# A new prologue for a fused graph-attention and hypergraph kernel on one core

## The chip, the cores and the metric

The kernel runs on one core of a Trainium2 chip. The metric is the device time of one execution in microseconds (us), lower is better. The engines are named as in the profile: PE (TensorE matmul), PEld (its weight loads), DVE (VectorE), ACT (ScalarE), POOL (GpSimd), SP (SyncE, which here only issues DMAs). "SPq" and "ACTq" are the queues that issue DMAs.

## What is computed

For 128 graphs of 128 nodes and 512 features, two layers, all in float32:

```
# layer 0: graph attention with 8 heads of 64 units
feats   = einsum(x, W)                       # per head
e       = leaky_relu(e_self[i] + e_neigh[j], 0.2) + (-1e10) * (1 - adj)
out     = relu(softmax(e) @ feats + b)       # heads side by side
x       = layernorm(x + out)
# layer 1: two hypergraph convolutions, H = (adj != 0), w = first row of adj
conv(v, W, b) = D^-1 H B^-1 H^T (v @ W^T) + b
h       = layernorm(relu(conv(x, W1, b1))) * gamma + beta
x       = layernorm(x + conv(h, W2, b2) + x)
```

e_self and e_neigh are dot products of each head's features with a_self and a_neigh. Since features are x times W, both can be had from x and a "score weight" (W times a_self, W times a_neigh): 16 extra columns.

## The kernel before

**Tiling.** A work item is a pair of graphs; there are 64 pairs (`PAIRS`). Nodes lie on the 128 partitions. Products of the later pairs (`feature`, `hidden`, `weigh`) combine the two graphs and the two halves of a weight in a seven-product (Strassen-like) scheme, `chain`; the weights therefore have derived blocks (`second_sums`, `prepare_hidden`, `prepare_output_block_sums`). Matmuls go in two column tiles of 64 (`columns`, L97).

**Order.** Everything is issued in one order that is written out by hand. Each step of a pair has a lag and a due time inside a period (`step`, `at`); the list `todo` adds preparation steps; `first` overrides due times of single steps of the first pairs; the whole list is sorted by due time (L1232) and issued in that order. [...] There are eight PSUM banks (`bank`), taken in turn. Due times are a sorting key only, in a unit of the author's.

**Steps of one pair.** Load adj, its first row, x and 32x32 blocks of both; `nodes` (inverse node degrees, L360 to L369) and `write_nodes`/`spread_nodes` (through DRAM to all partitions); `mask` (adj to 0 or -1e10, POOL L378); `x_transpose`; features (`pf`); `spread_rows` (the scores, one column per head, are turned into rows L542 and written to DRAM, `rd`) and `neighbours` (read back, spread over all partitions, `nb` L570); `masked` (POOL L589, adds the mask); `leaky` (ACT L605), `largest` (DVE L611), `exponential` (ACT L619), each per graph g and half of the heads q; `e_write`, `e_read` (through DRAM, `ed` and `eb`) and `e_transpose` (DVE L640); `attend` (`pav`, L677, L703), `attended`; `add_bias` (POOL L742, adds b0 to the features); `residual`, `rstds` (root on POOL, L767), `first_shift`/`first_output` (normalisation on ACT, L785 to L794); `edges`, `scale_edges`, `propagator` (`pd`), `r_evict` (`R`): the matrix D^-1 H B^-1 H^T; `propagate` (`pz`), `z_evict` (ACT L829), `z_sums` (POOL L840); `hidden` (`phX`, `phY`, `phW`), `h_sum` (DVE L866), `relu`, `square`; `weigh` (`py`), `y_scale`, `output` (`pq`), statistics and store.

**The prologue before.** Pairs 0 and 1 take other steps. w0 comes as four blocks; `prepare_first` copies each into a tile with two more columns per head, and fills these: the block times the broadcast a_self (DVE, L234) or a_neigh (POOL, L234), reduced per head on DVE (L238). x of both pairs is transposed on PE (`x_transpose_first`, L397, `px`), and `plain_features` (L523, `pf`) multiplies 264 columns per half: features and scores together. Pair 0's scores go through DRAM like those of all pairs (L550, L570). The transposes of pair 0's exponentials are on PE (L651, `pet`). `prepare_output` (L276, `pv`: 16 matmuls of two rows by 256 columns), `prepare_output_sums`, `prepare_output_spread` (L288, `gw` and `bw`) give sums that fold gamma, beta and the mean into w2; `prepare_output_blocks` (L300, 16 operations on DVE) scales w2 in place. pv, gw and bw stand ahead of `pz` of pair 0; half of L300 is done before or during it.

## Time and profile before

| what | value |
|---|---|
| runs | 2393.14, 2398.22, 2399.10 us; median 2398.22 |
| the profiled execution's own time | 2395.3 us |
| its span, first to last instruction | 2393.4 us |
| mean granted clock of PE | 0.996 |
| first transposes of x | 8.08 us |
| rows of pair 0 made, and read back on all partitions | 20.72 us, 27.94 us |
| first leaky of pair 0; last block of pav | 29.24 us; about 40.7 us |
| pz of pair 0, first product of phX | 47.23 us, 50.69 us |
| pfX of pair 2, pav of pair 1, pz of pair 1 | 64.92, 74.46, 87.06 us |
| HBM read and written | 239.08 MB, 102.73 MB |

How to read it: in the page, shares are of the span; the stretches give busy time per engine between two times; a chain of waits starts at the last instruction and is followed back, so that it names at each time the work that was last. A line of the timeline gives start, duration, engine, source line, operation, tile written <- tile read, shape and count, and in brackets the idle time of the engine before it with what ended it. fp32 matmuls appear as two passes (an x8 is four matmuls), transposes as one. L97 is the helper `columns`, so its rows are told apart by tile names.

### The profile page before, as it was taken

Reading aid. Unit: us, or ns where it says so; the run is one execution under the profiler, and the core shown is the slowest. Engines: PE = TensorE matmul, PEld = TensorE weight load, DVE = VectorE, ACT = ScalarE, POOL = GpSimd, SP = SyncE. Lnnn points to the kernel's source line nnn. Section 1 sums busy time; section 2 is a strip of 40 time slices with the busy share of each in tenths; the row PEclk is TensorE's granted clock in tenths of the full one; section 3 lists DMA queues with packets and bytes.
Section 4 is the critical chain, followed back from the end, with each engine's and each line's share of the span. In section 5 each row is a group of like instructions: output and inputs, shape, how many; then the busy total and the mean of one; then the engine's idle time right before and its main releaser. Section 6 shows DMA issues by size and latency. Waiting matters only on the chain.

```text
span 2393.4 us, 80729 instructions
## 1 busy us (share of the span) xinstructions
PE 2360.8 (99%) x32309; PEld 2026.8 (85%) x32309; DVE 2089.6 (87%) x4456; ACT 1528.5 (64%) x4481; POOL 1825.6 (76%) x2060
## 2 busy tenths in 40 slices
PE   7899999999999999999999999999999999999998
PEld 6788887888888888888888888888888888888886
DVE  7989888898898898898898888988988988988975
ACT  4565765756667667667667666666676676676662
POOL 5877786777877877877877778778778778778774
PEclk9999999999999999999999999999999999999999
DMA  6555454555554555555545555544545555555541
GB/s 197 133 148 150 143 144 134 159 143 147 151 148 144 149 148 148 151 143 154 144 142 157 141 147 155 146 146 147 150 143 153 147 150 139 148 156 140 149 128 37
DMA packets 431134, 347.09 MB, mean 145 GB/s; under 512 B 151440, under 2 KB 380328, under 8 KB 430760
## 3 DMA queue, kind: packets, MB, share of 16 engines
q1 hardware_dynamic: 427288, 337.46, 49.5%
q8 instruction: 256, 4.19, 0.7%
q10 hardware_dynamic: 3472, 4.47, 0.6%
q14 instruction: 118, 0.97, 0.2%
HBM read 239.08 MB, written 102.73 MB: 143 GB/s over the span
## 4 chain that ended last, share of the span: by engine, by line
PE 89%; DMA 4%; DVE 3%; ACT 1%; POOL 1%; issue 1%; SPq 1%; DVEq 0%; POOLq 0%; ACTq 0%
PE phX L97 17%; PE pyX L97 17%; PE pfX L97 8%; PE pyW L97 8%; PE phW L97 8%; PE pav L703 5%; PE phY L97 4%; PE pz L97 4%; PE pfW L97 4%; PE pq L97 4%; PE pyY L97 4%; PE pfY L97 2%; DMA ed<-nb 1%; PE pd L97 1%; DMA nb<-rd 1%
## 5 line engine op out<-in xcount | busy, mean ns | idle before, releaser
L344 ACT COPY py<-pyX 128x257 f32<-128x257 f32 x189 | 70.7, 374 | 538.5 <-PE pyX L97 465.6
L97 PEld LDWEIGHTS phX<-zS,w_sb 128*64 128x64 f32 x6144 | 350.6, 137 | 36.3 <-POOL ft L742 23.1
L97 PE MATMUL phX<-zS,w_sb 128*64 128x128 f32 x6144 | 373.4, 273 | 2.6 <-ACT ph L344 2.6
L904 POOL TENSOR_TENSOR sq<-sq 128x512 f32<-128x512 f32 (+2 forms) x384 | 343.9, 896 | 20.1
L589 POOL TENSOR_TENSOR nb<-nb,neg 128x512 f32<-128x512 f32 x256 | 319.9, 1284 | 23.1 <-DMA nb<-rd 12.7
L605 ACT ACTIVATE nb<-nb,ft 128x128 f32<-128x128 f32 x1020 | 325.1, 392 | 13.7 <-POOL nb L589 13.7
L619 ACT ACTIVATE nb<-nb,nm 128x128 f32<-128x128 f32 x1024 | 319.4, 392 | 4.2 <-DVE nm L611 4.0
L767 POOL TENSOR_TENSOR rso<-veo,mhalf 128x2 f32<-128x2 f32 x63 | 44.2, 701 | 338.4 <-DVE veo L765 338.4
L97 PE MATMUL pyX<-w_sb,hS 128*64 128x257 f32 x2016 | 245.1, 380 | 0.0
L97 PE MATMUL pyX<-w_sb,h 128*64 128x257 f32 x2016 | 243.7, 379 | 0.5 <-ACT py L344 0.5
L97 PE MATMUL pyW<-w_sb,hS 128*64 128x256 f32 x2016 | 243.3, 378 | 0.0
L881 ACT ACTIVATE h<-h,vecs 128x128 f32<-128x128 f32 x768 | 239.4, 394 | 2.0 <-DVE h L866 1.4
L611 DVE TENSOR_REDUCE nm<-nb 128x4 f32<-128x512 f32 x256 | 175.2, 684 | 48.8 <-ACT nb L605 46.2
L97 PEld LDWEIGHTS pyX<-w_sb,h 128*64 128x64 f32 x2016 | 173.7, 136 | 46.2 <-ACT py L344 0.9
L97 PEld LDWEIGHTS pyW<-w_sb,hS 128*64 128x64 f32 x2016 | 174.7, 136 | 43.6 <-issue 0.3
L742 POOL TENSOR_TENSOR ft<-ft,b_bc 128x512 f32<-128x512 f32 x128 | 203.9, 1613 | 6.1 <-ACT ft L533 6.1
L97 PEld LDWEIGHTS pyX<-w_sb,hS 128*64 128x64 f32 x2016 | 168.7, 137 | 38.7 <-issue 0.8
L640 DVE STREAM_TRANSPOSE eT<-eb 128x512 f32<-128x512 f32 x252 | 163.5, 685 | 5.7 <-DMA eb<-ed 4.7
L805 DVE SCALAR_TENSOR_TENSOR o<-y,b_bc 128x512 f32<-128x512 f32 x128 | 164.7, 1325 | 0.0
L1006 DVE SCALAR_TENSOR_TENSOR y<-y,rsh,bw_bc 128x512 f32<-128x512 f32 x126 | 150.1, 1229 | 14.9 <-POOL rsh L1002 14.9
L469 POOL TENSOR_TENSOR hS<-h 128x512 f32<-128x512 f32 x126 | 162.1, 1287 | 0.0
L892 ACT ACTIVATE sq<-h 128x512 f32<-128x512 f32 x256 | 160.6, 629 | 2.1
(178 smaller groups left out, 5672.4 us busy)
## 6 DMA issues: line engine op xcount, KB each, us to landing
nb<-rd SPq DMA_DIRECT2D x127, 512.0 KB, 5.6
ed<-nb SPq DMA_DIRECT2D x126, 512.0 KB, 3.4
eb<-ed SPq DMA_DIRECT2D x504, 128.0 KB, 2.9
x<-in_x_dram SPq DMA_DIRECT2D x64, 512.0 KB, 4.0
out_dram<-o SPq DMA_DIRECT2D x63, 512.0 KB, 2.9
xb<-in_x_dram SPq DMA_DIRECT2D x248, 128.0 KB, 5.5
a<-in_adj_dram SPq DMA_DIRECT2D x64, 128.0 KB, 2.4
w<-in_adj_dram SPq DMA_DIRECT2D x128, 64.0 KB, 5.0
```

The lines of the kernel that those rows point to most:

```text
L97: nc.tensor.matmul(to[rows], lhs[:, rows], rhs, start=start, stop=stop, skip_group_check=True)
L469: engine.tensor_tensor(t[:, i], in0, in1, op=op)
L589: nc.gpsimd.tensor_tensor(t, t, neg[:, :, None, :].to_broadcast([P, NB, HH, B]), op=ALU.add)
L605: nc.scalar.activation(t, t, AF.Prelu, bias=s["ft"][:, g, h, 0:1], alpha=SLOPE)
L611: nc.vector.tensor_reduce(s["nm"][:, g, hs], scores(p, s, g, hs).rearrange("p b h j -> p h b j"), AX.XY, ALU.max, negate=True,)
L619: nc.scalar.activation(t, t, AF.Exp, bias=s["nm"][:, g, h:h + 1])
L640: nc.vector.transpose(s["eT"][:, g, hs, :].rearrange("p h (b i) -> p h b i", b=NB), s["eb", g][:, :, hs, :].rearrange("p b h j -> p h b j"),)
L742: nc.gpsimd.tensor_tensor(t, t, b0_bc.rearrange("p (h u) -> p h u", h=H), op=ALU.add)
L805: nc.vector.scalar_tensor_tensor(s["o"][:, g, :], s["y"][:, g, :], 2.0, b2_bc, op0=ALU.mult, op1=ALU.add)
L881: nc.scalar.activation(dst[:, k, :], src[:, k, :], AF.Relu, bias=b1_sb[:, c:c + 1])
L892: nc.scalar.activation(s["sq"][:, g, q * KH // 2:(q + 1) * KH // 2, :], hid(s, g, q), AF.Square, scale=DH ** -0.5,)
L904: nc.gpsimd.tensor_tensor(t[:, :n, :], t[:, :n, :], t[:, n:2 * n, :], op=ALU.add)
```

## The change

Only steps of the first pairs and of the constants change; loops over pairs 2 to 63 stay as they are (apart from `blocked`, which loses the special layout of pair 0).

1. **Loads.** gamma, beta, b1, a_self and a_neigh come as 32 rows on ACT's queue; adj and its first rows of pair 0 first on SP, then w0 in four pieces of full rows, then x of pair 0 per graph. b0, w1, w2, the first row of pair 1 and the blocks of pair 2 are issued behind `spread_nodes` of pair 0, all on SP (before: w2 and half of w1 on ACT).
2. **Score weights.** w0 is transposed on PE (`first_transpose`), multiplied by a block matrix made of a_self and a_neigh in column tiles of 32 (`first_scores`), turned back (`first_scores_turn`) and added up by one reduction (`first_scores_out`). The copies of w0 into the wide tile and its four sums go from ACT and DVE to POOL.
3. **Scores as rows.** `x_scores` multiplies the score weights by x transposed, in four column tiles; `x_scores_turn` turns them into columns for the bias of `leaky`. `score_spread` puts pair 0's rows on all partitions by a matmul with a selection matrix (`heads`), and `first_masked` adds the mask while leaving PSUM. Pair 0 no longer goes through DRAM. Pair 1's rows still do, on ACT's queue.
4. **Attention of pair 0** is written out per graph and half; `first_root` and `first_normalize` take the root per graph and normalise on DVE instead of ACT.
5. **Features** of pairs 0 and 1 are products of 512 columns straight from `w0_raw`; two products of pair 1's graph 0 and all four of graph 1 stand after its attention scores, the last four behind `pz` of pair 0.
6. **Constants.** pv goes into four column tiles of 32 rows and stands behind pz and those features, its copy goes to ACT; gw stands behind phX's and phY's first products, bw behind the next; the 16 operations that scale w2 stand together behind gw.

The core of the diff:

```diff
+    for ap in (gamma, beta, b1, a_self, a_neigh):
+        rows = ap.rearrange("(k p) -> k p", p=P)
+        nc.scalar.dma_start(vec_rows[at_row:at_row + rows.shape[0]], rows)
+    load(0)
+    for k in range(KF):
+        load_first(k)
...
-            for c, bc in enumerate((as_bc, an_bc)):
...
-                (nc.vector, nc.gpsimd)[c].tensor_tensor(
-                    t, raw, bc[:, j * QU:(j + 1) * QU].rearrange("p (h u) -> p h u", h=HH)
-                    [:, None].to_broadcast([P, KF // 2, HH, U]), op=ALU.mult,
-                )
-                nc.vector.tensor_reduce(dst[:, :, :, c], t, AX.X, ALU.add)
...
+    def first_scores(k):
...
+        for c in range(KF):
+            nc.tensor.matmul(
+                made["pwa"][c * B:(c + 1) * B, k * P:(k + 1) * P], w0_a[:, c * B:(c + 1) * B],
+                made["wT", k // 2][:, k % 2, c], start=True, stop=True, skip_group_check=True,
+            )
...
     def prepare_first_sums():
-        second_sums(nc.vector, [w0_sb[:, i] for i in range(7)], w0_12)
+        second_sums(nc.gpsimd, [w0_sb[:, i] for i in range(7)], w0_12)
...
+        for n in range(2):
+            for j in range(2):
+                for c in range(NB):
+                    k = 2 * c + n
+                    blk = w2_blocks[2 * (k // (KH // 2)) + j][0]
+                    nc.tensor.matmul(
+                        t[c * B:(c + 1) * B, j * QU:(j + 1) * QU], gbs[:, k, :],
+                        blk[:, k % (KH // 2), :], start=(n == 0 and j == 0), stop=(n == 1),
...
     def prepare_output_sums():
...
+        made["sums"] = work.tile([P, F], F32, tag="sq", name="sums")
+        nc.scalar.copy(made["sums"], made["pv"])
...
+    def score_spread(p, s, g, q):
+        t = s["pn", g, q] = bank(f"pn_{g}{q}")
+        for h in range(HH):
+            nc.tensor.matmul(
+                t[:, h * N:(h + 1) * N], heads[:, q * HH + h, :], s["rows"][:, g], start=True,
...
+    def first_root(p, s, g):
...
+        nc.vector.tensor_scalar(ve, s["mv", "a"][:, g, 1:], EPS, None, op0=ALU.add)
+        nc.gpsimd.tensor_tensor(s["rs", "a"][:, g:g + 1], ve, mhalf[:, :1], op=ALU.pow)
...
+        (52.0, load_weights, (nc.sync, w1_blocks[:2], w1t, F // 2, HALF)),
+        (52.1, load_weights, (nc.sync, w1_blocks[:1:-1], w1t, F // 2, HALF)),
+        (52.2, load_weights, (nc.sync, w2_blocks, w2t, DH // 2, QU)),
...
-        (15.5, prepare_output_vectors, ()), (16.0, prepare_output, ()),
-        (78.3, prepare_rows, ()), (78.79, prepare_output_sums, ()),
-        (78.99, prepare_output_spread, (0, "gw")), (98.0, prepare_output_spread, (1, "bw")),
-        (98.1, prepare_output_bias, ()), (98.2, prepare_output_blocks, (slice(0, 1),)),
-        (99.75, prepare_output_blocks, (slice(1, 2),)),
-        (117.8, prepare_output_blocks, (slice(2, 3),)),
-        (118.1, prepare_output_blocks, (slice(3, 4),)),
+        (73.6, prepare_output_vectors, ()), (117.0, prepare_output, ()),
+        (117.05, prepare_output_sums, ()),
+        (119.7, prepare_output_spread, (0, "gw")), (121.65, prepare_output_spread, (1, "bw")),
+        (122.0, prepare_output_bias, ()), (119.75, prepare_output_blocks, (slice(0, 1),)),
+        (119.76, prepare_output_blocks, (slice(1, 2),)),
+        (119.8, prepare_output_blocks, (slice(2, 3),)),
+        (120.3, prepare_output_blocks, (slice(3, 4),)),
...
+        (1, 97.95, plain_features, 0, (2, 3)), (1, 116.8, plain_features, 1, (0, 1, 2, 3)),
```

L345 is the line of those 16 operations in the kernel after (L300 before); L389 its L344, L912 its L829.

## The prediction

> **What bounds the kernel now.** I read the page first, then stretches of the span cut at the first "propagate" matmul (pz of pair 0), then the chain of waits for the first 80 us, then the timeline around it. The page says TensorE (PE) is busy nearly all the time:

> ```profile
> PE 2360.8 (99%) x32309; PEld 2026.8 (85%) x32309; DVE 2089.6 (87%) x4456; ACT 1528.5 (64%) x4481; POOL 1825.6 (76%) x2060
> ```

> The edit touches only what is issued before about 125 us, so the stretches decide. Columns: stretch, its length, busy us of PE, weight load, VectorE (DVE), ScalarE (ACT), GpSimd (POOL), granted clock, DMA share, GB/s.

> ```profile
> 40.00:47.20 7.20, 3.18 (x32) 1.36 (x26) 6.86 (x19) 2.00 (x6) 2.50 (x4) 0.81 0.88 209
> 47.20:50.70 3.50, 3.47 (x33) 3.48 (x35) 3.40 (x13) 2.43 (x6) 2.93 (x6) 0.50 0.36 67
> 50.70:64.90 14.20, 13.40 (x234) 12.92 (x234) 14.10 (x27) 11.88 (x37) 10.18 (x10) 0.98 0.25 83
> 64.90:87.00 22.10, 20.94 (x236) 15.88 (x234) 21.58 (x36) 9.72 (x29) 21.52 (x18) 1.00 0.64 145
> 87.00:128.80 41.80, 37.24 (x509) 31.21 (x506) 38.52 (x92) 25.33 (x76) 29.54 (x35) 1.00 0.45 131
> 128.80:166.20 37.40, 36.78 (x510) 31.60 (x508) 32.08 (x71) 24.96 (x75) 30.34 (x34) 1.00 0.54 156
> ```

> To see: from 50.7 to 87 us DVE has no slack (14.10 of 14.20, 21.58 of 22.10), while PE loses about 2 us. The later pairs are PE's. The chain says the same: until 40 us it runs on PE, then on DVE.

> ```profile
> 8.08 1.96 PE px L397 x8
> 10.04 5.59 PE pf L523 x16
> ...
> 26.03 3.76 PE pf L523 x16
> 29.79 7.01 PE pv L276 x32
> 36.80 1.90 PE pet L651 x16
> ...
> 52.97 2.40 DVE w_sb L300 x6
> ...
> 58.88 2.10 DVE xT L385 x2
> 60.97 0.57 DVE h L866
> 61.54 0.33 DVE R L451
> 61.88 0.60 DVE nm L611
> ```

> The timeline shows where PE takes the next step from DVE (brackets: idle before, and who ended it):

> ```profile
> 63.12 1.73 PEld L97 LDWEIGHTS phW<-zT,w_sb 128*64 128x64 f32 x32 [0.35 <-DVE h L866]
> 63.12 1.97 PE L97 MATMUL phW<-zT,w_sb 128*64 128x128 f32 x32
> ```

> So this phW product waits for the second h sum. Whatever DVE must do between phX's start (50.69) and that sum moves everything later.

> [...] 8 transposes took 1.96 us at 8.08 and 1.12 at 15.47; after 4 idle us the 32 pz passes took 3.68 us, 1.94 one pair later. [...] Here two tiles of 64 (phX, 32 passes in 1.75 us, 0.055 each, against 0.123 for a 128-wide transpose) overlap; no 32-wide one is shown. [...]

> **Part by part.** Durations are rows of the timeline; a handover between engines is 0.2 us (px end to ACT copy). Matmuls count two passes: 264 columns cost 0.47 us per matmul at full clock, so 512 cost 0.9.

> *Score front.* Gone: 8 products with broadcast vectors (0.68 to 1.5 us each) and 8 reductions of 0.64. The four w0 pieces, by SP's issue costs (0.4 to 0.75 us each) behind adj and two first rows, should land at 5.4 to 7.7 us and x of pair 0 at 8.9 (7.94 today). DVE first does nodes (1.35), one reduction (0.25), edges and scaling (2.1): from about 5.0 to 8.7. Then wT copy 0.69, vectors and two placements 0.2 each: 10.0. Then everything alternates: scores 0.5, transposes 1.0, scores 0.5, DVE 0.69+0.42, turn 0.5, transposes 1.0, scores 0.5, ACT 0.59, scores 0.5, DVE 0.42, turn 0.5, px 2.0, ACT 0.59, ps 0.6, with the handovers: ps ends at 20.6 with PE at half clock, 17.8 at full. Then pf 1.8 (0.9), pn 2.0 (1.0), pst, two reductions 0.5, masked 0.69: the first leaky starts between 21.4 and 26.6. I take 24; today 29.24. Removing pair 0's DRAM trip (rows at 20.72, rows spread at 27.94) and four POOL masks (4.94) is worth these 5 us.

> *Attention of pair 0, from first leaky to last pav.* Today 29.24 to 40.71, 11.5 us. After: 8 leaky and 8 exponentials of graph 0 (5.2), the copy of features (0.6), bias on POOL (1.2, with handovers 7.3), pav, pet, eT copy, division and maximum (4 us on PE and DVE in turn) before graph 1's exponentials may start at 10.7; 1.2+0.6+1.2 later they end at 13.9. Graph 1's bias is queued on POOL behind the root of graph 0, which waits for residual, statistics and its own add (0.69+0.69+0.18+0.17 after 11.8): bias done 15.7, last pav ends 16.8. So 40.8: the 5 us are spent. Roots per graph cost the same 0.7 each and put this wait there.

> *Pair 1 and pz.* px 1.1, two ACT copies, ps, copy, pst: 3.5; half of pf 3.6 and pt 0.4: pz of pair 0 starts at 48.3 instead of 47.23. y is ready long before, so PE does not idle and pz costs 1.94 instead of 3.68.

> *Behind pz.* PE gets pf of graph 1 (3.6) and pv. pv's 16 matmuls take 7.2 us today; in four column tiles 1.8, if they overlap fully, 7.2 if not. Value taken 1.8. That path reaches phX at 55.6. But zT's copy is queued on ACT behind the first leaky of pair 1, which waits for rows (45.3), its DRAM write (3.0) and spread (4.9, both from the chain in later pairs), POOL mask 1.27, leaky 1.26: 55.9, and copy 0.6: phX starts at 56.6. **Shift +5.9.** [...] If the trip is 2 us shorter, pf and pv decide (55.6).

> *Constants on DVE.* Today 8 of the 16 scalings (L300, 0.41 each) are done or running at pz; from phX's start to the end of the h sum DVE takes 12.4 us. After: all 16 wait for gw, which stands behind phX and phY: 1.75+1.75+0.9+0.2 = 4.6. Then 16 x 0.41 = 6.6, maximum 0.68, xT 2.1, h 0.65, R 0.42, maximum 0.68, h 0.68: 11.8. Together 16.4, **+4.0**; the maximum and the adjacency step ahead of them, fed by the leaky behind the second zT copy, end 1.2 after gw: **+1.2**. phW starts at 74.2, not 63.12. Exponentials of pair 1, behind the last maximum, are as late, so its writes and pav are too.

> *At nothing:* w1, w2 and biases moved to SP behind dnb: 4 MB at about 200 GB/s end near 37 us, before phX; if x were behind them the front would slip, but x is ahead. First row of pair 1 and blocks of pair 2 follow them on SP, landing before 45 us; they are read at 46 and 70. First w0 sums moved to POOL (4 x 1.3) end near 24 and bias comes at 30; DVE loses 2.8 us there that it had free. Memsets: under 0.4 us each before 6 us. The adjacency step of pair 1 leaves the stretch behind pz (2.0) as 8 scalings enter (3.3): load nearly equal, and from pfX on the order is as before, so I see nothing that gives time back. PE idles some 4 us before phW, [...] left out of the point, kept in the range.

> **Sum.** 5.9 + 4.0 + 1.2 = 11.1. Own time of the profiled run 2395.3 (span 2393.4 and 1.9 around it) gives 2406.4. The median of the runs, 2398.2, is 2.9 above; I put the change on it: 2409.

> **Rivals.**
> *Same.* The clock is full from 14 us (leaky at 21.4, -2.6), the trip is short and pv ready (-1), the maximum is not late (-1.2): +6 and less, about 2402. For it: PE has work from 5 us. [...]
> *Column tiles do not overlap, or PE stays cold.* Up to 5.4 more for pv, 2.6 more for the front: about 2415. For it: no 32-wide tile in the trace. Against: the 64-wide ones overlap.
> *Faster.* One mechanism: DVE's queue behind phX is no longer last. Place: 47.2 to 128.8. Price: PE's idle time there, 0.8+1.2+4.6 = 6.6, and the slow pz, 1.7: 8.3 us, 2390. It decides if phX starts by 51 and DVE needs under 12.4 us for the stretch. For it: pf and pv now fill PE while y is made. Against: DVE gets 16 scalings after gw in that stretch.

> **Chances.** Main case 0.57 (2409), tiles or cold 0.12 (2415), same 0.21 (2402), faster 0.10 (2390). A measurement here tells 0.3% (7.2 us) from no change. Slower is the first two: 0.69; same 0.21; faster 0.10. Range: 2397 leaves out the faster case and a small part of the same one; 2420 is the main sum with serial pv and a cold array less a little: 2397 to 2420.

> **What would show it.** First leaky of pair 0 near 24 us; last pav near 41; pz near 48; phX's first product near 56 after a wait for zT; L345's 16 scalings in one block from 61 or 62; phW waiting for DVE near 74; the period after it unchanged. I am wrong if the first leaky comes before 18 us, if exponentials of graph 1 follow without a gap, if phX starts by 51, or if the scalings run while PE still has products.

## The result, and the profile after

The kernel after takes 2428.4 us (median of 4 runs, 2427.5 to 2432.1), the kernel before on the same chip 2396.4 (2393.1 to 2399.1): a ratio of 1.0137 with a 95% interval of 1.0119 to 1.0155. It is slower by 32 us; 11 were forecast, and 2428 lies outside the range of 2397 to 2420. The profiled execution took 2428.9 us, its span 2427.1.

The page's line of engine totals, first for orientation. PE's share of the span falls from 99% to 98%, and it carries 72 more matmul passes:

```profile
PE 2375.5 (98%) x32381; PEld 2003.8 (83%) x32381; DVE 2088.0 (86%) x4451; ACT 1526.3 (63%) x4480; POOL 1825.5 (75%) x2069
```

The stretches of the kernel after, cut at its own marks (pz of pair 0, first phX, pfX, pz of pairs 1, 2, 3; columns as before):

```profile
52.07:59.47 7.40, 7.40 (x74) 4.11 (x73) 7.16 (x19) 1.75 (x5) 6.11 (x8) 1.00 0.61 164
59.47:80.75 21.28, 17.09 (x240) 14.74 (x238) 18.42 (x36) 13.46 (x41) 11.42 (x11) 0.92 0.25 70
80.75:102.93 22.18, 20.99 (x236) 15.89 (x234) 21.69 (x36) 9.74 (x29) 21.60 (x18) 1.00 0.61 158
102.93:143.27 40.34, 37.21 (x507) 31.22 (x504) 38.87 (x90) 25.52 (x77) 30.59 (x35) 1.00 0.45 128
143.27:179.63 36.36, 36.36 (x506) 31.30 (x504) 32.43 (x70) 23.91 (x72) 28.46 (x33) 1.00 0.54 155
```

The stretch from phX to pfX grew from 14.20 to 21.28 us, and PE works 17.09 of it. From pfX on the stretches are as long as before or shorter (22.18 for 22.10, 40.34 for 41.80, 36.36 for 37.40). So up to here the picture is of the forecast kind, though the loss is larger. The chain of waits over the first 80 us (start, length, what) shows who was last:

```profile
1.73 5.94 DMA w<-in_adj_dram
...
12.99 0.66 PE pwa L258 x8
...
28.95 2.45 ACT eb L612 x8
...
60.92 3.51 DMA ab<-in_adj_dram
...
65.57 2.19 DVE deg L469
67.87 1.65 DVE w_sb L345 x4
...
73.26 1.56 DVE w_sb L345 x4
...
77.71 0.60 DVE nm L705
```

A load (the spread first rows), then the score front until the first leaky at 28.95, and later DVE with a load ahead of it (the adjacency blocks, ab), a node operation of two elements that took 2.19 us, and the scalings. The phW product behind them:

```profile
78.95 1.97 PE L97 MATMUL phW<-zT,w_sb 128*64 128x128 f32 x32 [0.37 <-DVE h L949]
```

But this is not where most of the 32 us went. The start of pz in each pair, after minus before, read from the timelines:

| pair | 0 | 1 | 2 | 10 | 13 | 20 | 30 | 41 | 50 | 62 | end of span |
|---|---|---|---|---|---|---|---|---|---|---|---|
| us | +4.8 | +15.9 | +14.5 | +8.3 | +9.1 | +11.1 | +13.4 | +20.8 | +25.6 | +35.3 | +33.7 |

The prologue costs 14.5 us up to pz of pair 2. By pair 10 some 6 us have come back, because the kernel before has irregular periods there (40.4 us in pair 8 alone). Then, in a loop whose steps are unchanged, 27 us are lost between pairs 10 and 62: before holds 36.37 us in every pair from 16 on, after has pairs of up to 38.6 among those of 36.37. Net of what came back, the loop is 19 of the 33.7 us.

Who waits in the loop is in the waits of SP's queue, 1500 to 2000 us of the span (us in total, times, longest; ed is the trip of the exponentials, rd that of the rows, sd that of some sums of the second layer). The kernel before:

```profile
SPq L631 <- DMA ed<-nb: 74.8, 26, 3.8
SPq L965 <- DMA sd<-sr: 19.7, 14, 2.8
SPq L570 <- DMA rd<-rows: 15.4, 14, 1.9
```

The kernel after:

```profile
SPq L725 <- DMA ed<-nb: 119.6, 27, 6.5
SPq L1048 <- DMA sd<-sr: 49.7, 14, 5.4
SPq L668 <- DMA rd<-rows: 32.6, 13, 2.9
```

The waits for all three trips through DRAM became longer, by 1.4 to 2.1 us each (119.6/27 for 74.8/26, and so on). In the page's chain of the whole execution, the share of DMAs rises from 4% to 16% and that of PE falls from 89% to 65%, so these waits are on the path. Bytes and DMA share are the same (145 GB/s at 0.51 between 535 and 2353 us, against 146 at 0.51), and so are durations on the engines. What remains open is why a 16 KB write lands later.

### The profile page after: what moved, and what is told of

It reads as the page before. It is cut to its first block, busy times and chain, and to the rows that moved or that the text cites. A ratio compares the mean times of both kernels' runs of the same rounds, so it can differ in the third digit from the quotient of the medians.

```text
span 2427.1 us, 80861 instructions
## 1 busy us (share of the span) xinstructions
PE 2375.5 (98%) x32381; PEld 2003.8 (83%) x32381; DVE 2088.0 (86%) x4451; ACT 1526.3 (63%) x4480; POOL 1825.5 (75%) x2069
## 4 chain that ended last, share of the span: by engine, by line
PE 65%; DMA 16%; DVE 6%; POOL 5%; ACT 4%; SPq 3%; issue 2%; DVEq 0%; POOLq 0%
PE pyX L97 13%; PE phX L97 11%; DMA ed<-nb 8%; PE pyW L97 7%; PE pfX L97 6%; PE phW L97 5%; PE pav L786 4%; PE pz L97 4%; PE pyY L97 3%; DMA nb<-rd 3%; PE phY L97 3%; PE pfW L97 3%; PE pq L97 3%; DMA eb<-ed 3%; SPq L725 2%
## 5 line engine op out<-in xcount | busy, mean ns | idle before, releaser
L389 ACT COPY py<-pyX 128x257 f32<-128x257 f32 x189 | 70.7, 374 | 552.6 <-PE pyX L97 477.3
L97 PEld LDWEIGHTS phX<-zS,w_sb 128*64 128x64 f32 x6144 | 350.4, 137 | 41.6 <-POOL ft L825 22.8
L97 PE MATMUL phX<-zS,w_sb 128*64 128x128 f32 x6144 | 373.6, 273 | 6.0 <-ACT ph L389 6.0
L691 POOL TENSOR_TENSOR nb<-nb,neg 128x512 f32<-128x512 f32 x252 | 314.6, 1281 | 64.9 <-DMA nb<-rd 50.0
L699 ACT ACTIVATE nb<-nb,ft 128x128 f32<-128x128 f32 x992 | 316.9, 392 | 30.7 <-POOL nb L691 30.3
L850 POOL TENSOR_TENSOR rso<-veo,mhalf 128x2 f32<-128x2 f32 x63 | 44.1, 700 | 337.9 <-DVE veo L848 337.9
L97 PE MATMUL pyX<-w_sb,hS 128*64 128x257 f32 x2016 | 243.6, 379 | 0.0
L97 PE MATMUL pyX<-w_sb,h 128*64 128x257 f32 x2016 | 243.1, 379 | 0.5 <-ACT py L389 0.5
L97 PE MATMUL pyW<-w_sb,hS 128*64 128x256 f32 x2016 | 242.8, 378 | 0.0
L97 PEld LDWEIGHTS pyX<-w_sb,h 128*64 128x64 f32 x2016 | 168.8, 136 | 51.1 <-ACT py L389 0.9
L97 PEld LDWEIGHTS pyW<-w_sb,hS 128*64 128x64 f32 x2016 | 171.7, 136 | 46.4 <-issue 0.3
L97 PEld LDWEIGHTS pyX<-w_sb,hS 128*64 128x64 f32 x2016 | 165.9, 136 | 40.1
```

What stands on the lines that cost most here:

```text
L97: nc.tensor.matmul(to[rows], lhs[:, rows], rhs, start=start, stop=stop, skip_group_check=True)
L691: nc.gpsimd.tensor_tensor(t, t, neg[:, :, None, :].to_broadcast([P, NB, HH, B]), op=ALU.add)
L699: nc.scalar.activation(t, t, AF.Prelu, bias=own, alpha=SLOPE)
```

## Experiments

"Before" in a ratio is the kernel before on the same chip. PE instructions are the page's matmul passes and weight loads plus waits.

**Does the place in memory do it?** After has its DRAM scratch 16 KB lower from pair 1 on (pair 0's rows are gone), and its SBUF tiles lie in another order. Four kernels exchange one of the two.

a_dram, from the kernel after:

```diff
-        s["dd"] = dram.tile([NB, B, B], F32, tag="dd", name=f"dd_d_{p}")
+        s["dd"] = dram.tile([(1, 2)[p == 0] * NB, B, B], F32, tag="dd", name=f"dd_d_{p}")[-NB:]
```

> The kernel after, with the DRAM scratch of all pairs moved up by 16 KB, to the addresses that it has in the kernel before (pair 0's node tile is twice as long; nothing else changes). Theory of scratch addresses: the round trips through DRAM are longer in the loop because every scratch tile of pairs 1 to 63 lies 16 KB lower. Then pairs 13 to 62 cost 36.37 us each again, the growth of 26.8 us between pair 10 and pair 62 goes, and the time is about 2402. Theory of SBUF placement: no change, 2428. Theory of lost slack (the later start leaves SP's transfers less room, wherever the data lie): no change, 2428.

b_dram, from the kernel before:

```diff
-        rd = s["rd"] = dram.tile(shape, F32, tag="rd", name=f"rd_{p}")
+        if p == 1:
+            rd = st[0]["rd_flat"].rearrange("(b c j) -> b c j", b=NB, c=B)
...
+        s["rd"] = rd
```

> The kernel before, with the DRAM scratch from pair 1 on 16 KB lower, as in the kernel after (pair 1's rows use pair 0's tile again). Theory of scratch addresses: the prologue stays as it is, and the loop loses some 25 us as in the kernel after: about 2421. Theory of SBUF placement: no change, 2396. Theory of lost slack: no change, 2396.

a_sbuf and b_sbuf, each with the other kernel's order of tags:

```diff
+    pad = const.tile([P, 8], F32, name="pad")
+    nc.gpsimd.memset(pad[:1, :1], 0.0)
+    for n, (tag, bufs, size) in enumerate((
+        ("y2", 1, 1028), ("eb", 2, 1024), ("eb", 2, 1024), ("eT", 1, 2048),
...
+    )):
+        t = work.tile([P, size], F32, tag=tag, name=f"place_{n}", bufs=bufs)
+        (nc.gpsimd, nc.vector)[n % 2].memset(t[:1, :1], 0.0)
```

> The kernel after, with its working tiles in SBUF laid out in the order and at the addresses of the kernel before (41 one-element memsets on POOL and DVE at the start claim the places; up to 3 us at the start). Theory of SBUF placement: the loop's growth of 26.8 us goes, about 2402 to 2405. Theory of scratch addresses: 2428 to 2431. Theory of lost slack: 2428 to 2431.

> The kernel before, with its working tiles in SBUF laid out in the order of the kernel after (within 64 bytes; 43 one-element memsets at the start, up to 3 us). Theory of SBUF placement: the loop loses some 25 us, 2421 to 2425. Theory of scratch addresses: 2396 to 2399. Theory of lost slack: 2396 to 2399.

Measured: 2427.3, 2398.6, 2436.5 and 2393.1 us (ratios 1.0125, 1.0004, 1.0162, 0.9980). Each kernel keeps its own loop: growth against before between pairs 10 and 62 is 23 and 31 us in the two made from after, and there is none from pair 16 to 60 beyond 1.2 us in the two made from before (b_dram loses 1.8 us more in pair 60). Neither place is the cause. That a_sbuf is 8 us slower still is not explained.

**What differs then?** A row trip is the time from the issue of a pair's row write (rd) to that of its read-back (nb). Row trips are short or long in whole runs of pairs, not at random. In the kernel before, those of pairs 2 to 14 are mostly 2.6 to 3.3 us and nearly all later ones 1.45; in the kernel after it is the other way round, short up to pair 12, but for 2.2 us in pair 11, and 2.2 to 3.3 from 13 on. Something else passes slowly through the period. The list of DMA queues holds a candidate. After, with packets, MB and share:

```profile
q8 instruction: 256, 4.19, 0.7%
```

These are 256 reads of 16 KB. The trace has 65,677 PE instructions (two times 32381 and 915 that compute nothing, nearly all of them waits), 256.5 per read, and between 150 and 2250 us 256.2 of them start from one read to the next on average. So these look like PE's own instructions, some 256 in a read; that is an estimate from the counts alone, and the runs below test it. The records spread the reads over the whole execution, four in nearly every pair. Nine in ten take 0.9 to 1.4 us. Their starts, in us after the pair's pz (from the trace's DMA records):

```
pair        before                        after
20          1.94  9.17  17.48  26.63      7.44  14.23  25.70  35.75
35          2.47  9.32  20.58  26.92      0.78   9.12  14.82  25.87
```

The row write is issued at 25.1 to 25.4 in both. In pair 35 of the kernel after, a read starts at 25.87 and lasts 1.23 us. 120 of the row write's 128 packets start by 26.42, the last 8, a sixteenth, between 27.09 and 27.22. Before, all have started by 26.19, and the read comes behind them. The loop as a whole shows the same late sixteenth: the trace has sixteen landing signals for each row write, and where a read starts within 1 us of the write's issue (47 of the pairs 2 to 61 of the kernel after), fifteen of them have come 1.49 us after the issue and the last one 2.82 us after it (medians); without such a read, in 53 pairs of the kernel before, it is 1.42 and 1.44. How a read delays that one share is not shown, as the records don't say what moved a packet. The queue's timeline shows the price: write issued, read-back issued (start and length of the issue), pair 35 of before and of after.

```profile
1361.11 0.34 SPq L552 DMA_DIRECT2D rd<-rows  x1
1362.64 1.53 SPq L570 DMA_DIRECT2D nb<-rd  x2
```

```profile
1378.29 0.34 SPq L658 DMA_DIRECT2D rd<-rows  x1
1381.18 0.94 SPq L668 DMA_DIRECT2D nb<-rd  x2
```

1.53 us against 2.89. If one read is 256 PE instructions, as the counts say, then where in the period the reads fall is set by how many PE instructions stand ahead of the loop, and the new prologue has 140 more (72 passes, 72 weight loads, 4 waits fewer; 65,677 for 65,537 in the traces). This can be tested.

**Test: move only the reads.** The next five kernels add idle PE instructions at the start, ahead of the first data, with the zero tile and the PSUM bank that they need, and nothing else (n = 23, 64, 12 for a_f92, a_f256, a_f48; 35 and 58 for b_f140, b_f232; each matmul is four instructions):

```diff
+    idle = const.tile([P, B], F32, name="idle")
+    nc.vector.memset(idle, 0.0)
+    t = bank("idle")
+    for _ in range(n):
+        nc.tensor.matmul(t[:B, :8], idle, idle[:, :8], start=True, stop=True)
```

> The kernel after, with 92 PE instructions that compute nothing needed (23 matmuls of 32x8 zeros) at the start, where PE waits for data. Theory of instruction reads: PE's own instructions come from memory in 16 KB pieces, 256 of them, four per pair; [...] in pairs 13 to 62 of the kernel after they fall on the writes of rows and exponentials, whose last share then comes about 1.4 us late. Where in the period they fall is set by how many PE instructions stand ahead of the loop: 140 more in the kernel after than before. With 92 more, the reads fall where those of the kernel before fell in its quiet pairs: row trip 1.5 us in nearly all pairs, no growth between pair 10 and 62, 2400 to 2404. Theory of lost slack (the late start alone leaves the transfers no room): 2428, growth as before.

> Control: the kernel after with 256 such PE instructions at the start, one whole 16 KB piece, so that the reads fall at the same places of the period as in the kernel after. Theory of instruction reads: the loop's growth stays, 2426 to 2431 [...]. Theory that the added work itself helps (a warm array, another order of banks): as fast as with 92.

> The kernel before with 140 idle PE instructions at the start, as many as the kernel after has more ahead of its loop. Theory of instruction reads: pairs 2 to 12 become quiet (4 to 6 us won), pairs 13 to 62 get the long trips of the kernel after (some 26 us lost): 2414 to 2422. Theory of lost slack: 2396, the loop starts as early as before.

> The kernel before with 232 idle PE instructions at the start, so that the reads that fall on the trips of its pairs 3 to 14 fall elsewhere from pair 2 on. Theory of instruction reads: the irregular periods of pairs 5 to 15 (5.6 us over 36.37 in the sum) go, 2390 to 2393. Theory of lost slack: 2396.

> The kernel after with 48 idle PE instructions at the start, about half of 92. Theory of instruction reads: the reads move through the period by about 2 instructions per pair (with 92 more, long row trips begin at pair 59 and not at pair 12), so that with 48 they begin near pair 36, the loss grows from there on, and half of the 25 us is left: 2411 to 2418. Theory that any idle work at the start wins it (or that one threshold is crossed): 2403, or 2428.

Measured. "Hit" is a pair in which a read starts within 1 us of the row write's issue; "excess" is the sum of the periods over 36.37 us:

| kernel | PE instructions ahead, against before | excess, pairs 2 to 15 | hits in pairs 16 to 60 | row trip, hit / not | excess, pairs 16 to 60 | median us (ratio, 95%) |
|---|---|---|---|---|---|---|
| before | 0 | 7.1 | 0 of 45 | - / 1.54 | 0.0 | 2396.4 |
| after | +140 | 2.3 | 43 | 2.84 / 3.22 | 25.2 | 2428.4 (1.0119 to 1.0155) |
| b_f140 | +140 | 1.7 | 44 | 2.84 / 3.12 | 19.0 | 2409.0 (1.0035 to 1.0084) |
| a_f256 | +396 | 3.6 | 45 | 2.73 / - | 25.8 | 2426.7 (1.0100 to 1.0167) |
| a_f48 | +188 | 0.3 | 24 | 2.72 / 1.51 | 8.5 | 2411.0 (1.0033 to 1.0067) |
| a_f92 | +232 | 0.0 | 2 | 2.82 / 1.53 | 3.3 | 2403.4 (1.0027 to 1.0044) |
| b_f232 | +232 | 1.1 | 3 | 2.80 / 1.54 | 0.3 | 2389.7 (0.9964 to 0.9980) |

A shift of 140 makes the kernel before lose 19 us in its own loop, though that loop starts no later (pz of pair 2 at 127.3 us, 128.8 before), so a late start is not what does it. A shift by a whole read (256) leaves the kernel after as it was, so that idle work as such, the other bank order and a busier array are not the cause. Against that run, on the same chip, 92 wins 23 us (2426.7 to 2403.4), and nearly all of it in the loop: ahead of pair 2 both have won about the same (2.8 and 2.6). With 48 the long trips begin at pair 38 (without idle work at pair 13, with 92 at pair 59: about 2 instructions of drift per pair), as the theory said, and the time, 2411.0, is at the lower edge of what was expected. The number of reads follows PE's count as well: 257 instead of 256 in the three runs with 232 or more instructions ahead. And the chain of each page goes with the hits: DMAs hold 17% of it in a_f256 and 12% in b_f140, but 1% in a_f92 and 2% in b_f232.

Not all is explained. b_f140 came out 5 us below its expected range: at the same shift the kernel after loses 6 us more in pairs 16 to 60 (25.2 for 19.0), and why is open. The waits of SP's queue in a_f92, in the stretch shown above:

```profile
SPq L731 <- DMA ed<-nb: 89.7, 27, 5.7
SPq L1054 <- DMA sd<-sr: 35.3, 14, 5.1
SPq L674 <- DMA rd<-rows: 16.2, 14, 2.1
```

The wait for the row trip is back at 1.2 us (1.1 before, 2.5 after). The other two came back in part: 3.3 us for the exponentials (2.9 and 4.4), 2.5 for sd (1.4 and 3.6), and the periods there stay at 36.4 us nonetheless, but for pair 51 (39.0 us, most of the 3.3 us of excess, unexplained). b_f232 beats both kernels: it is the kernel before with 58 idle matmuls.

**The prologue.** Six kernels take it apart, all with the 92 idle instructions, so that the loop is quiet. The first four build on one another. The c runs, the d runs and a_f92 come from three chips, so that their totals compare by the ratios:

c_root:

```diff
-        (0, 68.2, first_root, 1), (1, 68.4, plain_features, 0, (0, 1)),
+        (0, 67.9, first_root, 1), (1, 68.4, plain_features, 0, (0, 1)),
```

> The kernel after with 92 idle PE instructions (2403.4 us, quiet loop), and the root of graph 1 of pair 0 issued ahead of pair 1's score turn (its first DVE operation waited 1.7 us behind two reductions that wait for PE). Queue theory: the propagate product of pair 0 (pz) starts at 49.9 instead of 51.57, and pair 1's by as much earlier than 100.43: 2401.7. Rival, that DVE's queue behind pz decides alone (its 16 scalings wait for the adjacency blocks, not for pz): pz of pair 0 moves and that of pair 1 does not: 2403.

c_hid, with the edit of c_root:

```diff
-        (79.0, prepare_hidden, (nc.gpsimd, 0)), (79.1, prepare_hidden, (nc.gpsimd, 1)),
+        (58.7, prepare_hidden, (nc.gpsimd, 0)), (58.71, prepare_hidden, (nc.gpsimd, 1)),
```

> As the one before, and the two sums of w1 on POOL, which lie beside the last normalisation on DVE (2.57 us where graph 0's took 1.21), issued some 13 us earlier. Theory that a big POOL sum holds up DVE's operation: the normalisation takes 1.2 us again, pz of pair 0 at 48.5, 2400.3. Rival, that the 2.57 us has another cause: it stays, and nothing is won over the one before.

c_gw, with the edits of c_hid; the four slices of `prepare_output_blocks` go from 119.75, 119.76, 119.8 and 120.3 to 69.6, 69.7, 73.56 and 73.57:

```diff
-        made["sums"] = work.tile([P, F], F32, tag="sq", name="sums")
+        made["sums"] = work.tile([P, F], F32, tag="xS", name="sums")
...
-        (73.6, prepare_output_vectors, ()), (117.0, prepare_output, ()),
-        (117.05, prepare_output_sums, ()),
-        (119.7, prepare_output_spread, (0, "gw")), (121.65, prepare_output_spread, (1, "bw")),
+        (45.3, prepare_output_vectors, ()), (66.7, prepare_output, ()),
+        (66.75, prepare_output_sums, ()),
+        (68.15, prepare_output_spread, (0, "gw")), (121.65, prepare_output_spread, (1, "bw")),
```

> As the one before, and pv, gw and the 16 scalings of w2 put ahead of and around pz of pair 0 (pv behind the transposes of pair 1's x, scalings behind the last normalisation and behind pair 1's nodes), where PE and DVE have free time. Theory of the DVE block, as predicted for the kernel after (16 scalings between phX and phW cost 4.0 us and more, pv ahead of phX 1.9): phW of pair 0 starts by 67 to 69 instead of 76.15, pz of pair 1 by 92 to 95, total 2393 to 2397. Rival, that DVE's whole load up to 100 us is what counts and moving it changes nothing: pz of pair 1 not earlier than in the one before, about 97, total 2400.

c_all, with the edits of c_gw:

```diff
-            todo.append((p * T + (28.5 if p == 2 else 20.5), load_edges, (p,)))
+            todo.append((70.2 if p == 2 else p * T + 20.5, load_edges, (p,)))
...
-        ("r_evict", 0): 62.9, ("add_bias", 0, 0): 58.6, ("add_bias", 0, 1): 64.0,
+        ("r_evict", 0): 62.9, ("add_bias", 0, 0): 58.6, ("add_bias", 0, 1): 62.7,
```

> As the one before, and the adjacency blocks of pair 2 loaded some 4 us earlier, and the bias of pair 0's graph 1 on POOL ahead of the root of graph 0. Theory: the wait for the blocks goes (1.4 us in the kernel after), the bias lets the last attention products start 1.2 us earlier: 1 to 2.5 us less than the one before. Rival: both waits are covered by DVE's queue, no change.

d_front, from a_f92; d_both is c_all with this edit and `prepare_hidden` back at 79.0 and 79.1:

```diff
-        ("nodes", 0): 43.7, ("write_nodes", 0): 45.0, ("spread_nodes", 0): 51.0,
-        ("mask", 0): 43.6, ("edges", 0): 44.2, ("scale_edges", 0): 44.3, ("propagator", 0): 61.0,
+        ("nodes", 0): 51.05, ("write_nodes", 0): 51.08, ("spread_nodes", 0): 60.45,
+        ("mask", 0): 43.6, ("edges", 0): 51.06, ("scale_edges", 0): 51.07, ("propagator", 0): 61.0,
```

> The kernel after with 92 idle PE instructions (2403.4, first leaky of pair 0 at 28.45), and DVE's node and adjacency work of pair 0 put behind the copy of pair 0's score rows, its spread behind the weights on SP. Theory of the front: the copies that feed the score weights no longer wait for the first rows, w0's first block is copied some 2.8 us earlier, first leaky near 25.7, last attention products and pz of pair 0 earlier by as much (51.57 to 48.8), total 2400.6. Rival, that PE at half clock and w0's landing set the front: first leaky after 27.5, total 2403.

> The last one of the earlier chain (root ahead, pv, gw and scalings early, adjacency blocks and bias early: 2397.8) with the node work behind the score rows and with the two sums of w1 on POOL back at their place behind the last normalisation. If the front and POOL's sums add up: pz of pair 1 at 92 to 94 (96.5), 2393 to 2396. Rival, that POOL's sums there hold up DVE as in the kernel after (some 1.3 us twice): pz of pair 1 at 95 or later, 2397.

| kernel | first leaky | last pav | pz of pair 0 | pz of pair 1 | pz of pair 2 | median us (ratio to before, 95%) |
|---|---|---|---|---|---|---|
| a_f92 | 28.45 | 44.0 | 51.57 | 100.43 | 140.50 | 2403.4 (1.0027 to 1.0044) |
| c_root | 29.09 | 44.7 | 52.21 | 100.78 | 141.13 | 2403.1 (1.0015 to 1.0034) |
| c_hid | 29.61 | 46.2 | 56.21 | 103.54 | 144.37 | 2404.9 (1.0021 to 1.0039) |
| c_gw | 29.10 | 45.8 | 55.91 | 99.11 | 139.45 | 2401.1 (1.0007 to 1.0021) |
| c_all | 28.91 | 44.1 | 53.55 | 96.50 | 136.28 | 2397.8 (0.9991 to 1.0010) |
| d_front | 29.22 | 48.5 | 60.24 | 107.61 | 147.96 | 2409.8 (1.0031 to 1.0061) |
| d_both | 29.10 | 47.3 | 57.89 | 99.84 | 139.89 | 2402.2 (1.0008 to 1.0026) |

*c_root* missed: the root came 1.0 us earlier, pz did not. Pair 1's features stand ahead of pz on PE (from 48.46, for 47.82 in a_f92), and pz started behind them at 52.21; the wait on DVE lay beside that.

*c_hid* confirmed what holds up DVE and still lost 4 us at pz of pair 0 (its total is not clear of c_root's). Last normalisation of pair 0 with POOL's sum beside it (kernel after) and without (c_hid):

```profile
49.41 2.35 POOL L306 TENSOR_TENSOR w_sb<-w,w_sb 128x1024 f32<-128x1024 f32 x1
49.48 2.57 DVE L853 TENSOR_SCALAR y<-y,mva,rsa 128x512 f32<-128x512 f32 x1 [0.48 <-POOL rsa L640]
```

```profile
51.37 0.51 DVE L859 TENSOR_SCALAR y<-y,mva,rsa 128x512 f32<-128x512 f32 x1
```

The operation took 0.51 us alone. Beside a POOL operation it ended 0.3 us behind it in each case seen: graph 0's (43.62 behind 43.33) and graph 1's (52.05 behind 51.76) in the kernel after, graph 1's in c_root, and graph 1's in d_both (55.55 behind 55.27). But pz came at 56.21: with the sums beside pair 0's attention that ended later, and transposes of pair 1's x then took 1.98 us instead of 1.23, at a granted clock of 0.54 (44.4 to 47.0 us). The clock was at half a second time from 51.4 to 54.8 (0.68 granted between 50.8 and 56.2).

*c_gw* moves pz of pair 1 by 4.4 us against c_hid, with pz of pair 0 within 0.3: pv, gw and the scalings off the way between phX and phW are worth that, and the idea that only DVE's total counts falls. It stays short of 92 to 95 us, since it starts from a pz of pair 0 as late as in c_hid (PE at half clock from 44.1 to 47.5, 8 transposes in 1.95 us), and DVE waited 1.74 us for the adjacency blocks. *c_all* takes that wait away and wins 2.6 us more at pz of pair 1, a little above what was expected. But its pz of pair 0 is already 2.4 us earlier, with the bias moved and no half clock there (8 transposes in 1.23 us), so the blocks by themselves are not shown to be worth anything. Its phW starts 6.2 us earlier than in the kernel after, without a wait for DVE:

```profile
72.75 1.92 PE L97 MATMUL phW<-zT,w_sb 128*64 128x128 f32 x32
```

*d_front* missed. With DVE free, the first block of w0 was copied at 10.46 instead of 11.7, and the score rows' product started at 21.36 instead of 22.50. The rest is w0's landing (first transpose at 9.31) and PE at half speed (1.91 us for 8 transposes of x). The first leaky was not earlier, since the node work now stood ahead of the reductions of the scores. And its spread, now behind eight weight loads on SP, was waited for:

```profile
45.33 0.43 DVE L499 TENSOR_TENSOR R<-pd,dnb 128x256 f32<-128x256 f32 x1 [1.93 <-DMA dnb<-dd_d]
...
46.49 2.00 PE L766 MATMUL pav<-ft,eT 128*64 128x65 f32 x32 [2.28 <-DVE eT L639]
```

From this wait on (45.6 to 59.3) PE ran at half clock (8 transposes of pair 1's x in 1.98 us at 48.43, 1.23 in c_root), and from last pav to pz it took 11.7 us instead of 7.5.

*d_both* has the same wait (pz of pair 1 at 99.84) and says nothing on the sums of w1 alone.

## Why the prediction was wrong, point by point

**The step that failed** is "from pfX on the order is as before, so I see nothing that gives time back", with "the period after it unchanged" as its sign. The order was unchanged and the period was not. The step counted what the change does to the engines' queues and not what 140 more PE instructions do to the place of PE's instruction reads. That term is some 25 us of excess in pairs 16 to 60, and moving the reads alone takes 23 us off the median (a_f256 to a_f92), nearly all of them in the loop. The step was wrong in its other direction too: 6 us came back by pair 10, as the reads that had disturbed pairs 3 to 14 of the kernel before moved away (b_f140 shows the same, 1.7 us of excess there for 7.1). With the reads at the same place, 232 instructions on, the two kernels differ by 13.7 us (a_f92 and b_f232): that is what the forecast 11.1 can fairly be laid against, though the idle work itself takes 2.8 us off the first kernel's way to pair 2 and adds 0.2 to the other's.

**The sum for the prologue** was 11.1; pfX stands 15.8 later. Its terms:

- *Score front*, "I take 24": 28.95. The working gave 26.6 with PE at half clock and 21.4 at full, and 24 lay between. PE was at half clock until 27.1, by the durations (see below), which is 2.6 of the 5 us. The rest is late loads: the working took DVE's placements to be done by 10.0, and the scores started at 12.99, as DVE's node work waited for the spread rows until 7.69 and w0's first block came at 8.98, not between 5.4 and 7.7. In d_front, with DVE free, they still started at 12.04, so that most of it is w0's landing. From there to the end of the score rows it took 10.4 us, for 10.6 in the working. The rows of that sum add up to 10.3, so that the handovers of 0.2 it names are hardly in it, and the match is in part luck: some of the products ran beside copies.
- *Attention of pair 0*: 16.8 forecast, 15.6 measured, 1.2 us in the change's favour, with the gap on POOL's bias behind the root as said (1.02 us of PE waiting for it). (Its 7.3 and 4 make 11.3, where the sum went on with 10.7; graph 1's exponentials started after 9.8.)
- *Pair 1 and pz*: 7.5 us from last pav to pz forecast, 7.5 measured (44.5 to 52.07). The forecast 48.3 was early by the front, less those 1.2.
- *pv in column tiles*: 1.8 forecast, 1.9 measured (57.6 to 59.5), where the same 32 passes, two rows wide, took 7.0 in the kernel before (29.72 to 36.79): the 32-wide tiles overlapped.
- *phX*, to start at 56.6 because zT's copy is queued on ACT: it started at 59.5, when pf and pv were through; the copy was done at 58.6. Write and spread took 6.5 us (49.03 to 55.55), not 7.9, so that the path by pf and pv decided, which the prediction had kept open. Shift 8.8 instead of 5.9, by the front.
- *Constants on DVE*, +4.0 and +1.2: from phX to phW 19.5 us instead of 17.6. The mechanism is as forecast (16 scalings in one block behind gw, c_gw wins 4.4). The scalings began 3.6 us after gw (64.2 to 67.87) instead of 1.2; what followed took 11.0 for 11.8. Not counted: DVE waited 1.4 us for the adjacency blocks, whose load had moved behind pair 1's nodes on SP, and spent 2.18 us in a node operation of 128x2 beside a POOL sum (0.17 for the shortest of the twelve in the first 400 us). PE's idle time before phW came (3.82 us), and at its end the clock went to half (74.8 to 78.3, a phX product of 3.49 us, 1.92 for the one before it). That cost nothing here, as DVE was busy until phW's start.

Of the rivals, the cold half of "tiles or cold" came true (2.6 us in the front), the other half did not: the column tiles overlapped. That its 2415 has a prologue of about the right size is in part chance, since the late loads stand in it for pv's 5.4. "Same" had counted on a full clock from 14 us on.

**The clock of the front.** In a view of stretches the granted clock reads 1.00 for the first 27 us of the kernel after. But the trace has no clock record before 27.1 us there, and the view counts time without a record as 1.00. The durations tell: the eight passes of the first line took 0.24 us each, the 24 of the second 0.12.

```profile
25.24 1.91 PE L595 MATMUL pn<-sT,heads 128*128 128x128 f32 x8
27.77 2.84 PE L595 MATMUL pn<-sT,heads 128*128 128x128 f32 x24
```

In the kernel before the records begin at 13.8 us, just where the passes of pf go from 0.65 to 0.39 us. Why PE stayed at half clock so long, no run shows.

**The sign** held, and the 0.69 on it, and it would have held with the reads out of the way (a_f92 is 8 us slower than before). But 19 of the 33.7 us of span came from what was left out, and that they fell on the slow side was luck of the instruction count.

## What to carry to other kernels

When a loop that was not edited changes its pace, compare its DMA round trips pair by pair before looking for a new wait: if long and short trips come in runs of iterations, look at when the instruction reads fall (2.72 us with one near the write, 1.51 without, in a_f48). A prologue's instruction count can be worth 1% here, so compare two versions of a prologue at equal phase (here modulo 256 PE instructions: 2426.7 us with 256 more, 2428.4 without, 2403.4 with 92), or the one measures the other's luck. A step that is moved takes its loads along: both misses on SP (adjacency blocks in the change, node spread in d_front) were loads put behind others. And look where a trace's clock records begin: ahead of the first one (27.1 us in the kernel after) a granted clock of 1.00 says nothing, and equal products must be compared by their durations.
